# Four graph layers on one core: scores in halves over four banks, weighted sums in one piece, jobs placed by a table

## The chip, the cores and the metric

The kernel runs on one core of one Trainium2 chip. The metric is the device time of one execution in microseconds (us), the median of several runs. One profiled execution is shown beside it, as recorded by the hardware profiler. TensorE is PE in the views, VectorE is DVE, ScalarE is ACT, GpSimd is POOL and SyncE, which here only issues DMAs, is SP.

## The reference

There are 32 batch elements of 512 nodes with 64 features, float32, and one sparse 512x512 matrix `adj`. Four graph layers follow each other, each added to its input after layer norm and relu:

```python
h = relu(layernorm(x)); x = x + L0(h, adj)   # 3 steps: v = relu([v, adj@v] @ W1.T + b1) @ W2.T + b2
h = relu(layernorm(x)); x = x + L1(h, adj)   # 2 steps: z = relu((adj@z) @ W[i])
h = relu(layernorm(x)); x = x + L2(h, adj)   # graph attention, 8 heads of 128, and an output layer of the same form
h = relu(layernorm(x)); x = x + L3(h, adj)   # additive attention

def gat_layer(x, graph, W, b):               # L2: each head, and the output layer
    h = x @ W
    s = einsum('bnd,bmd->bnm', h, h) * graph
    s = where(s == 0.0, -1e16, s)
    a = softmax(s, axis=2)
    return einsum('bnm,bmd->bnd', a, h) + b

# L3: e = leaky_relu(e_src[:, :, None] + e_dst[:, None, :], 0.2) * adj (diagonal 1); softmax; a @ h + bias
```

Almost all the work lies in the attention: for each element eight heads and one output layer of L2, and one of L3, each with a softmax over 512x512 scores.

## The kernel before

**Pairs and units.** Two batch elements (a pair) are worked on together, their 2 x 64 features side by side in 128 partitions. There are 16 pairs. The layers L0 and L1 of a pair are `front(p)`, a Python generator that is advanced step by step. The attention of a pair is cut into ten units: eight `Heads` (element j, two heads each: q = 0 to 3), one `Out` (the output layer of L2 for both elements) and one `Last` (L3). Each unit has a tile `sm` of eight blocks of 128x512 scores.

**What a unit does**, by method:

- `scores(k)`, k = 0 to 3: two blocks. `gram` makes them on TensorE, two banks of `s`, from `Y` (or `HH`) and `ZZ` (L400), and adds -1e16 where the graph has no edge by a bf16 product with `NEGM` (L403). `by_graph` (L417, VectorE) multiplies a block by the graph into `sm` and takes each row's maximum `mx`; `negate` (L424, POOL) makes `nmx` of two blocks. In `Last` the scores come from `pd` (L637) and a Prelu on ACT (L640) writes them into `sm`.
- `exponentials(k)` (L428, ACT): two blocks, with row sums `ssum`.
- `normalise(k)`: a reciprocal of two sums on VectorE (L438), two multiplications on POOL (L440).
- `turn(k)` (L446, VectorE): two blocks are transposed in 32x32 squares.
- `weigh` (L454, TensorE): 16 x 8 matmuls of tiles 32x64 sum the values weighted by the softmax, into four banks `u`. A float32 matmul stands as two instructions in the profile, so a unit has 256.
- Later stages of a `Heads` unit: `evict` (L501, ACT) copies `u` to `us`; `apply_w` multiplies by the head's weights into `py` (L481) and applies a Prelu into `y` (L491); each second unit has `project` (L508, TensorE), whose result is added into `cat` (L517 and L519, VectorE); the last unit of an element has `features` (L524) and `nodes` (L534). `Out` and `Last` have an eviction of their own, then transposes (L551), residual sums, and in `Out` the layer norm and the inputs of `Last`.
- `keys` (L683, TensorE, into `pk`; L691, ACT, into `Y`) prepares the left sides of two units' scores.
- `quarters` issues 16 DMAs on SP that lay values out for `weigh`.

**Groups and lags.** The order of all jobs is written out by hand. Each unit starts at a group number g0, and a tick is four groups. `scores(k)` stands at g0 + k, `exponentials(k)` one later, `normalise(k)` two, `turn(k)` three. `weigh` comes in three chunks of 6, 5 and 5 of its 16 steps at g0 + 9, 10, 11, the eviction and `apply_w` at g0 + 12. A step of the next pair's front stands at certain groups (`FRONT_AT`). Within a group `ORDER` says which kind goes first:

```python
ORDER = ("begin", "norm", "turn", "evict", "s", "keys", "exp", "w", "full", "front", "av", "o")
```

Engines take their instructions in this order, each from its own queue. A pair takes ten ticks; `Out` and `Last` of a pair run among the heads of the next one. The first front runs alone, ahead of everything.

**PSUM.** Eight banks: two for `s` (and `pd`), four in two fixed tiles of two banks (`u`; `py` in the first of them, `pk` in the second), two for all other products (`mm`). `sm` has three buffers.

Of the kernel before, what the change touches and what calls it, by code (L numbers as in the profile page):

```python
# [8 lines left out]
F32 = mybir.dt.float32  # L9
# [5 lines left out]
P = 128  # L15
# [6 lines left out]
def gnn_stack_kernel(  # L22
# [56 lines left out]
    ap_ = ctx.enter_context(tc.tile_pool(name="ap", bufs=3))  # L79
    hp = ctx.enter_context(tc.tile_pool(name="hp", bufs=2))  # L80
    st = ctx.enter_context(tc.tile_pool(name="st", bufs=6))
    ps_s = ctx.enter_context(tc.tile_pool(name="ps_s", bufs=2, space=bass.MemoryType.PSUM))
    ps_u = ctx.enter_context(tc.tile_pool(name="ps_u", bufs=1, space=bass.MemoryType.PSUM))
    ps_m = ctx.enter_context(tc.tile_pool(name="ps_m", bufs=2, space=bass.MemoryType.PSUM))

    def mm_ps():
        return ps_m.tile([P, N], F32, tag="mm", name="mm")

    def two_banks(k, name):

        return ps_u.tile([P, 2, N], F32, tag=f"u{k}", name=name)
# [194 lines left out]
    def aggregated(v, pe, first=True):  # L286

        for m in range(NT):
            if m == 2:
                yield  # L290
            nc.tensor.matmul(  # L291
                pe,
                lhsT=v[:, m].rearrange("p j d -> p (j d)"),
                rhs=AT[:, m, :],
                start=(first and m == 0),
                stop=(m == NT - 1),
            )
# [8 lines left out]
    def front(p, state):  # L306
# [11 lines left out]
        hT = transposed(v, "hT0", 1)  # L318
        yield
        for step in range(STEPS):  # L320

            k = min(step, 1)
            pv = by_nodes(hT, W1T[:, 1, k, :])
            v = lp.tile([P, NT, 2, D], F32, tag="v", name="v")
            if step == 0:
                nc.scalar.copy(v, pv)
            else:
# [5 lines left out]
                )  # L333
            ph = mm_ps()
            nc.tensor.matmul(ph, lhsT=W1T[:, 0, k, :], rhs=hT, start=True, stop=False)  # L335
            yield
            yield from aggregated(v, ph, first=False)
            hT = lp.tile([P, N], F32, tag="hT0", bufs=1, name="hT0")
# [10 lines left out]
        for i in range(LAYERS):  # L349
            pe = mm_ps()  # L350
            yield from aggregated(z, pe)
# [13 lines left out]
        state[p] = {"x2": x2, "z": z, "ZQ": [None, None], "ZZ": [None, None]}  # L365
# [17 lines left out]
    class Unit:  # L383
# [10 lines left out]
        def gram(self, k, operands):  # L394
# [6 lines left out]
            for half in range(2):  # L401
                for ab in range(2):
# [6 lines left out]
                    )  # L409
            for half in range(2):  # L410
                s = 2 * k + half
                self.by_graph(s, pss[half], A2[:, s, :])
            self.negate(k)
# [22 lines left out]
        def normalise(self, k):  # L436
            two = slice(2 * k, 2 * k + 2)
            nc.vector.reciprocal(self.rs[:, two], self.ssum[:, two])  # L438
            for s in range(2 * k, 2 * k + 2):
# [8 lines left out]
        def weigh(self, jbs):  # L448
            if jbs.start == 0:
                self.u = [two_banks(k, "u") for k in range(2)]  # L450
            for jb in jbs:
                for c in range(2):
                    for i in range(4):
                        nc.tensor.matmul(  # L454
                            self.u[i // 2][R[c], i % 2, 0:P],
# [6 lines left out]
    class Heads(Unit):  # L462
# [12 lines left out]
        def apply_w(self):  # L475

            py = two_banks(0, "py")
            for ab in range(2):
                for c in range(2):
                    for r in R:  # L480
                        nc.tensor.matmul(  # L481
                            py[r, c, ab * N // 2 : (ab + 1) * N // 2],
# [4 lines left out]
                        )  # L487
            for ab in range(2):
                h = 2 * self.q + ab
                y = hp.tile([P, 2, N // 2], F32, tag="y", bufs=6, name="y")  # L490
                nc.scalar.activation(  # L491
                    y, py[:, :, ab * N // 2 : (ab + 1) * N // 2], AF.Prelu, bias=cols[:, h : h + 1], alpha=0.01
                )
                state[self.p].setdefault("y", []).append(y.rearrange("p c n -> p (c n)"))

        def stages(self):

            def evict():
                self.us = hp.tile([P, 2, NT // 2, P], F32, tag="us", name="us")
                for ab in range(2):  # L500
                    nc.scalar.copy(self.us[:, ab], self.u[ab][:, :, 0:P])  # L501

            def project():
                s = state[self.p]
                pa = mm_ps()
                for k in range(2):
                    for ab in range(2):
# [6 lines left out]
                        )  # L514
                if self.q == 1:
# [23 lines left out]
            sts = {0: [("evict", evict)]}  # L539
            if self.q % 2 == 1:  # L540
                sts[4] = [("o", project)]
            if self.q == NQ - 1:
                sts[6] = [("full", features)]
                sts[7] = [("full", nodes)]
# [12 lines left out]
    class Out(Unit):  # L557
# [12 lines left out]
        def stages(self):  # L570
            s = state[self.p]

            def evict():

                self.yT = hp.tile([P, N], F32, tag="us", name="yT")
                for ab in range(2):
                    nc.scalar.activation(
                        self.yT[:, ab * N // 2 : (ab + 1) * N // 2].rearrange("p (s i e) -> p i s e", i=2, e=32),
                        self.u[ab][:, :, 0:P].rearrange("p i (s e) -> p i s e", e=32),
# [28 lines left out]
            def nodes():  # L608
# [10 lines left out]

            return {  # L620
                0: [("evict", evict)], 1: [("full", residual)], 2: [("full", norm)], 3: [("full", norm)],
                4: [("full", norm)], 5: [("full", features)], 6: [("full", weights)], 7: [("full", nodes)],
            }

    class Last(Unit):
# [5 lines left out]
        def scores(self, k):  # L631
# [6 lines left out]
            for i in range(2 * k, 2 * k + 2):  # L638
                t = i % NT
                nc.scalar.activation(  # L640
                    self.sm[:, i, :], self.pd[j], AF.Prelu, bias=s["src"][:, t, j : j + 1], alpha=0.2
                )
                self.by_graph(i, self.sm[:, i, :], A3[:, t, :])
            self.negate(k)
# [4 lines left out]
        def stages(self):  # L649
            s = state[self.p]  # L650

            def evict():
                self.yT = hp.tile([P, N], F32, tag="us", name="yT")
                yT = self.yT.rearrange("p (t k i e) -> p k i t e", k=2, i=2, e=32)
                for k in range(2):
                    nc.scalar.activation(
                        yT[:, k],
                        self.u[k][:, :, 0:P].rearrange("p i (t e) -> p i t e", e=32),
# [14 lines left out]
            return {0: [("evict", evict)], 1: [("full", residual)]}  # L673

    def keys(ua, ub):
# [3 lines left out]
        py = two_banks(1, "pk")  # L679
        for ab in range(2):  # L680
            for par in range(2):
                for half, un in enumerate((ua, ub)):
                    nc.tensor.matmul(  # L683
                        py[R[par], half, ab * N // 2 : (ab + 1) * N // 2],
# [4 lines left out]
                    )  # L689
        Y = hp.tile([P, 2, N], F32, tag="Y", name="Y")  # L690
        nc.scalar.copy(Y.rearrange("p u n -> p (u n)"), py.rearrange("p u n -> p (u n)"))  # L691
# [5 lines left out]
    state = {}  # L697
    for _ in front(0, state):
        pass

    LAG_V, LAG_E = 9, 12
    CHUNKS = (range(0, 6), range(6, 11), range(11, 16))
# [105 lines left out]
```

## Time and profile before

| | us |
|---|---|
| median of 3 runs | 2603.95 (2600.87 to 2606.08) |
| the profiled execution: its own time | 2606.89 |
| its span, first to last instruction | 2604.0 |
| PE busy in the span | 2419.7 |
| VectorE busy | 1883.9 |
| ACT busy | 1487.2 |
| POOL busy | 1292.3 |
| granted TensorE clock, mean | 0.972 |

The page of a profile has the busy time of each engine, the span in 40 slices, the DMA queues, the chain of work that ended last (followed back from the last instruction to whatever released each step), and the costliest groups of instructions by line, with the idle time of the engine ahead of them. The timeline lists instructions in order of time, equal ones merged. Matmuls are pipelined, so the length of a group on PE overlaps the next one; the difference of two starts is what a group takes. Busy time per engine by stage, in windows of 156 us between 260 and 2288 us, is nearly constant: PE 149.6 to 150.9, VectorE 116.6 to 119.5, ACT 92.8 to 94.9, POOL 80.7 to 82.2.

### The profile page before, as it was taken

The page shows a single profiled execution, that of the slowest core. Times are in us where ns is not written, and L with a number is a line of the kernel's source. Part 1 is how long each engine was busy: PE and PEld are TensorE (multiplying, and loading weights), DVE is VectorE, ACT ScalarE, POOL GpSimd, SP SyncE. Part 2 cuts the span into 40 slices and gives each one's busy share as a digit, 9 for nine tenths or more (in the row PEclk, how much of TensorE's full clock was granted, in tenths as well). Part 3 has the DMA queues.
Part 4 walks back from the last instruction along what each step waited for, and adds up shares of the span by engine and source line. Part 5 has one row for each costly group of instructions (what it writes and reads, how often), then busy time and mean ns, then how long its engine had stood idle before and what let it go on. Part 6 is the DMA issues. An engine that isn't in the chain of part 4 may idle for free.

```text
span 2604.0 us, 120934 instructions
## 1 busy us (share of the span) xinstructions
PE 2419.7 (93%) x54020; PEld 1340.8 (51%) x54020; DVE 1883.9 (72%) x4390; ACT 1487.2 (57%) x3601; POOL 1292.3 (50%) x2162
## 2 busy tenths in 40 slices
PE   5798999999999999999999999999999999999984
PEld 3344555555555555555555555555555555555552
DVE  3457677877867787786777778677777868778853
ACT  0345565565656556575655656566565655657652
POOL 1335454645545465554545545465554546555522
PEclk9899999999999999999999999999999999999986
DMA  3101011020211102021120201112020110202011
GB/s 77 18 6 27 15 26 32 17 41 12 40 23 25 34 14 41 15 38 25 22 37 10 45 15 34 29 18 40 7 44 19 30 29 14 42 5 43 17 34 26
DMA packets 260748, 70.74 MB, mean 27 GB/s; under 512 B 257660, under 2 KB 258692, under 8 KB 260228
## 3 DMA queue, kind: packets, MB, share of 16 engines
q1 hardware_dynamic: 258944, 62.82, 13.6%
q8 instruction: 422, 6.91, 1.2%
q14 instruction: 98, 0.80, 0.1%
q10 hardware_dynamic: 1284, 0.21, 0.1%
HBM read 8.40 MB, written 4.19 MB: 5 GB/s over the span
## 4 chain that ended last, share of the span: by engine, by line
PE 85%; ACT 7%; DVE 3%; POOL 2%; issue 1%; DMA 1%; SPq 1%; ACTq 0%; POOLq 0%
PE u L454 25%; PE s L400 22%; PE mm L291 12%; PE s L403 5%; PE mm L508 5%; PE mm L303 4%; PE py L481 3%; ACT sm L428 3%; ACT sm L640 2%; PE mm L335 2%; PE pk L683 1%; PE mm L524 1%; PE mm L534 1%; DVE sm L417 1%; POOL r L249 1%; PE mm L551 1%
## 5 line engine op out<-in xcount | busy, mean ns | idle before, releaser
L428 ACT ACTIVATE sm<-sm,nmx 128x512 f32<-128x512 f32 x1280 | 915.0, 721 | 236.7 <-POOL nmx L424 236.7
L417 DVE CUSTOM_DVE_ANT_0 sm<-s,A 128x512 f32<-128x512 f32 x1152 | 744.0, 682 | 360.2 <-PE s L403 359.5
L440 POOL TENSOR_SCALAR sm<-sm,rs 128x512 f32<-128x512 f32 x1280 | 879.5, 700 | 221.7 <-DVE rs L438 218.3
L454 PE MATMUL u<-sm,vq 32*64 32x128 f32 x40960 | 750.2, 282 | 106.4 <-ACT y L491 48.2
L454 PEld LDWEIGHTS u<-sm,vq 32*64 32x64 f32 x40960 | 631.1, 134 | 351.9 <-issue 167.6
L446 DVE STREAM_TRANSPOSE sm<-sm 128x1024 f32<-128x1024 f32 x640 | 784.6, 1226 | 16.3 <-POOL sm L440 15.9
L424 POOL TENSOR_SCALAR nmx<-mx 128x2 f32<-128x2 f32 x640 | 154.0, 241 | 930.4 <-DVE mx L417 589.4
L400 PE MATMUL s<-ZZ,Y 64*64 64x512 f32 x4096 | 603.3, 618 | 13.1 <-DVE mx L417 13.0
L403 PE MATMUL s<-NEGM,I2b 64*64 64x512 bf16 x2304 | 263.3, 379 | 0.0
L428 ACT ACTIVATION_READ_ACCUMULATOR sm<-sm,nmx 128x1 f32 x1280 | 249.8, 195 | 0.0
L400 PEld LDWEIGHTS s<-ZZ,Y 64*64 64x64 f32 x4096 | 127.9, 132 | 189.2 <-DVE mx L417 66.4
L501 ACT COPY us<-u 128x256 f32<-128x256 f32 x256 | 83.4, 381 | 238.8 <-PE u L454 238.8
L291 PE MATMUL mm<-AT,v 128*128 128x512 f32 x384 | 188.2, 614 | 0.0
L438 DVE RECIPROCAL rs<-ssum 128x2 f32<-128x2 f32 x640 | 101.5, 159 | 113.8 <-ACT sm L428 113.0
L491 ACT ACTIVATE y<-py,cols 128x512 f32<-128x512 f32 x256 | 161.7, 685 | 8.2 <-PE py L481 2.8
L403 PEld LDWEIGHTS <-I2b 64*64 64x64 bf16 x2304 | 83.4, 108 | 159.3 <-issue 158.4
L481 PE MATMUL py<-us,Wh 64*64 64x256 f32 x2048 | 136.3, 379 | 5.9 <-ACT us L501 5.9
L291 PE MATMUL mm<-AT,z 128*128 128x512 f32 x256 | 127.3, 622 | 8.1 <-DVE z L253 7.4
L508 PE MATMUL mm<-y,Wo_sb 128*64 128x512 f32 x512 | 124.0, 605 | 0.0
L417 DVE CUSTOM_DVE_ANT_0 sm<-sm,A 128x512 f32<-128x512 f32 x128 | 93.4, 766 | 34.2 <-ACT sm L640 34.2
L249 POOL TENSOR_TENSOR r<-ve,mhalf 128x8 f32<-128x8 f32 x64 | 106.1, 1657 | 22.7 <-DVE ve L247 11.8
L291 PEld LDWEIGHTS mm<-AT,v 128*128 128x128 f32 x384 | 65.5, 189 | 97.7 <-issue 76.7
(124 smaller groups left out, 1870.1 us busy)
## 6 DMA issues: line engine op xcount, KB each, us to landing
vq<-z SPq DMA_DIRECT2D x512, 32.0 KB, 1.9
vq<-hn SPq DMA_DIRECT2D x512, 32.0 KB, 1.9
vq<-h3n SPq DMA_DIRECT2D x512, 32.0 KB, 1.9
xt<-in_x_dram SPq DMA_DIRECT2D x32, 128.0 KB, 3.3
out_dram<-xo SPq DMA_DIRECT2D x32, 128.0 KB, 2.1
A<-in_adj_dram SPq DMA_DIRECT2D x3, 1024.0 KB
Wh<-in_L_gnn_Wh_dram SPq DMA_DIRECT2D x2, 256.0 KB, 3.8
Wo_sb<-in_L_gnn_W_out_dram SPq DMA_DIRECT2D x1, 256.0 KB
```

Of the source, the lines that this page charges most:

```text
L291: nc.tensor.matmul(pe, lhsT=v[:, m].rearrange("p j d -> p (j d)"), rhs=AT[:, m, :], start=(first and m == 0), stop=(m == NT - 1),)
L400: nc.tensor.matmul(pss[half][R[ab], :], lhsT=lhsT, rhs=rhs, start=True, stop=False)
L403: nc.tensor.matmul(pss[half][R[ab], :], lhsT=I2b[R[half], :], rhs=NEGM[R[half], k, :], start=False, stop=True,)
L417: nc.vector.tensor_tensor_reduce(self.sm[:, s, :], src, graph, 1.0, -FMAX, ALU.mult, ALU.max, self.mx[:, s : s + 1])
L424: nc.gpsimd.tensor_scalar(self.nmx[:, two], self.mx[:, two], -1.0, None, ALU.mult)
L428: nc.scalar.activation(self.sm[:, s, :], self.sm[:, s, :], AF.Exp, bias=self.nmx[:, s : s + 1], accum_out=self.ssum[:, s : s + 1],)
L440: nc.gpsimd.tensor_scalar(self.sm[:, s, :], self.sm[:, s, :], self.rs[:, s : s + 1], 1.0, ALU.mult, ALU.mult)
L446: nc.vector.transpose(out=two, in_=two)
L454: nc.tensor.matmul(self.u[i // 2][R[c], i % 2, 0:P], lhsT=self.values(i, c)[32 * i : 32 * i + 32, jb, :], rhs=self.sm[32 * i : 32 * i + 32 ...
L481: nc.tensor.matmul(py[r, c, ab * N // 2 : (ab + 1) * N // 2], lhsT=Wh2[R[c], 2 * self.q + ab, r], rhs=self.us[R[c], ab].rearrange("p i (s ...
L491: nc.scalar.activation(y, py[:, :, ab * N // 2 : (ab + 1) * N // 2], AF.Prelu, bias=cols[:, h : h + 1], alpha=0.01)
L508: nc.tensor.matmul(pa[R[ab], :], lhsT=Wo_sb[:, 2 * (self.q - 1 + k) + ab, :], rhs=s["y"].pop(0), start=(k == 0), stop=(k == 1),)
```

## The change

PSUM is divided otherwise: four banks for `s`, four for `mm`, and `u`, `py` and `pk` are now `mm` tiles of one bank each, in turn with all other products. `sm` has two buffers instead of three. A unit's scores are made in two halves of two Gram products (places s0, s1 and s2, s3); the maxima are jobs of their own, one for each block (r0 to r7). `normalise` takes four blocks with one reciprocal (nA, nB). `weigh` is one piece of 256 instructions, and `aggregated` in the front one piece of four matmuls. Since every tile is one bank, evictions come in more and smaller instructions. `apply_w`, `project` and `keys` become generators, so that the matmuls and the eviction have places of their own (w and y, o and c, k and Y); front steps are split likewise, 25 in all (F0 to F24: F3 transposes, F4 / F7 / F10 the product by nodes, F5 / F8 / F11 its copy, F6 / F9 / F12 the aggregation, F14 and F21 mean and squares, F15 and F22 variance and power). The table `PLACES` gives each job a tick, counted from its unit's or pair's own, and a place within the tick; jobs of a tick run in order of their places. The fronts of the first two pairs run together ahead of everything: seven steps of the second among those of the first. All heads now start at consecutive ticks 0 to 3 and 5 to 8, `Out` of the pair before at tick 4 and `Last` at tick 9. The numbers of matmuls are the same.

```diff
-    ap_ = ctx.enter_context(tc.tile_pool(name="ap", bufs=3))
+    ap_ = ctx.enter_context(tc.tile_pool(name="ap", bufs=2))
...
-    ps_s = ctx.enter_context(tc.tile_pool(name="ps_s", bufs=2, space=bass.MemoryType.PSUM))
-    ps_u = ctx.enter_context(tc.tile_pool(name="ps_u", bufs=1, space=bass.MemoryType.PSUM))
-    ps_m = ctx.enter_context(tc.tile_pool(name="ps_m", bufs=2, space=bass.MemoryType.PSUM))
+    ps_s = ctx.enter_context(tc.tile_pool(name="ps_s", bufs=4, space=bass.MemoryType.PSUM))
+    ps_m = ctx.enter_context(tc.tile_pool(name="ps_m", bufs=4, space=bass.MemoryType.PSUM))
...
         for m in range(NT):
-            if m == 2:
-                yield
             nc.tensor.matmul(
...
             for half in range(2):
-                s = 2 * k + half
-                self.by_graph(s, pss[half], A2[:, s, :])
-            self.negate(k)
+                self.pss[2 * k + half] = pss[half]
+
+        def maxima(self, s):
+            self.by_graph(s, self.pss.pop(s), A2[:, s, :])
+            if s % 2 == 1:
+                self.negate(s // 2)
...
-        def normalise(self, k):
-            two = slice(2 * k, 2 * k + 2)
-            nc.vector.reciprocal(self.rs[:, two], self.ssum[:, two])
-            for s in range(2 * k, 2 * k + 2):
+        def normalise(self, ks):
+            ss = slice(2 * ks.start, 2 * ks.stop)
+            nc.vector.reciprocal(self.rs[:, ss], self.ssum[:, ss])
+            for s in range(ss.start, ss.stop):
...
-        def weigh(self, jbs):
-            if jbs.start == 0:
-                self.u = [two_banks(k, "u") for k in range(2)]
-            for jb in jbs:
+        def weigh(self):
+            self.u = [mm_ps() for _ in range(4)]
+            for jb in range(N // 32):
...
-            py = two_banks(0, "py")
+            py = [mm_ps() for _ in range(2)]
...
+            yield
             for ab in range(2):
...
-                nc.scalar.activation(
-                    y, py[:, :, ab * N // 2 : (ab + 1) * N // 2], AF.Prelu, bias=cols[:, h : h + 1], alpha=0.01
-                )
+                for c in range(2):
+                    nc.scalar.activation(
+                        y[:, c],
+                        py[c][:, ab * N // 2 : (ab + 1) * N // 2],
...
-                for ab in range(2):
-                    nc.scalar.copy(self.us[:, ab], self.u[ab][:, :, 0:P])
+                for i in range(4):
+                    nc.scalar.copy(self.us[:, i // 2, i % 2], self.u[i][:, 0:P])
...
-        nc.scalar.copy(Y.rearrange("p u n -> p (u n)"), py.rearrange("p u n -> p (u n)"))
+        for half in range(2):
+            nc.scalar.copy(Y[:, half, :], py[half])
...
-    state = {}
-    for _ in front(0, state):
-        pass
+    state = {p: {} for p in range(NPAIR)}
+    first, second = front(0, state), front(1, state)
+    HEAD = 7
+    for n, _ in enumerate(first):
+        if 4 <= n < 4 + HEAD:
+            next(second)
+
+    PLACES = {
+        "begin": (0, 0), "s0": (0, 4), "s1": (0, 5), "r0": (0, 6), "r1": (0, 10), "r2": (0, 14),
+        "r3": (0, 16), "x0": (0, 23), "x1": (0, 27), "nA": (0, 45), "s2": (0, 50), "s3": (0, 55),
+        "r4": (0, 57), "r5": (0, 59), "r6": (0, 62), "r7": (0, 63), "x2": (0, 70), "x3": (1, 3),
+        "t0": (0, 66), "t1": (0, 68), "nB": (1, 17), "t2": (1, 43), "t3": (1, 44), "av": (1, 69),
+        "us": (2, 2), "w": (2, 46), "y": (2, 47), "k": (-1, 48), "Y": (-1, 49), "o01": (3, 34),
+        "c01": (3, 38), "o03": (4, 30), "c03": (4, 36), "o11": (3, 12), "c11": (3, 33), "o13": (3, 30),
+        "c13": (3, 35), "f0": (5, 21), "h0": (5, 65), "f1": (5, 28), "h1": (5, 60), "or": (2, 20),
+        "oA": (2, 32), "oB": (2, 49), "oC": (2, 67), "oT": (3, 18), "oW": (3, 54), "oN": (4, 42),
+        "lr": (2, 37), "ZZ1": (0, 9), "ZQ1": (0, 61), "F0": (-2, 30), "F1": (-2, 64), "F2": (-2, 67),
+        "F3": (-1, 11), "F4": (-1, 15), "F5": (-1, 22), "F6": (-1, 40), "F7": (-1, 52), "F8": (-1, 53),
+        "F9": (0, 56), "F10": (2, 7), "F11": (2, 8), "F12": (2, 31), "F13": (3, 26), "F14": (3, 39),
+        "F15": (4, 1), "F16": (4, 29), "F17": (5, 41), "F18": (6, 13), "F19": (6, 51), "F20": (7, 24),
+        "F21": (7, 25), "F22": (7, 58), "F23": (7, 67), "F24": (8, 19),
+    }
...
+    def place(unit, t):
+        at(t, "begin", unit.begin)
+        for k in range(4):
+            at(t, f"s{k}", lambda k=k: unit.scores(k))
+            at(t, f"x{k}", lambda k=k: unit.exponentials(k))
+            at(t, f"t{k}", lambda k=k: unit.turn(k))
+        for s in range(NS):
+            at(t, f"r{s}", lambda s=s: unit.maxima(s))
+        at(t, "nA", lambda: unit.normalise(range(0, 2)))
+        at(t, "nB", lambda: unit.normalise(range(2, 4)))
+        at(t, "av", unit.weigh)
+        for names, fn in unit.stages():
+            parts(t, names, fn)
...
-            for group in ORDER:
-                for gr, fn in todo:
-                    if gr == group:
-                        fn()
-            assert g not in jobs
-            g += 1
+            for _, fn in sorted(jobs.pop(t, []), key=lambda job: job[0]):
+                fn()
+            t += 1
```

## The prediction, made before the changed kernel ran

> **What bounds the kernel now.** I read the page from the top: engines, then the chain that ended last, then TensorE's timeline over one pair of batch elements in the middle, where every pair looks alike.
>
> ```profile
> span 2604.0 us, 120934 instructions
> PE 2419.7 (93%) x54020; PEld 1340.8 (51%) x54020; DVE 1883.9 (72%) x4390; ACT 1487.2 (57%) x3601; POOL 1292.3 (50%) x2162
> ...
> PE 85%; ACT 7%; DVE 3%; POOL 2%; issue 1%; DMA 1%; SPq 1%; ACTq 0%; POOLq 0%
> ...
> L454 PE MATMUL u<-sm,vq 32*64 32x128 f32 x40960 | 750.2, 282 | 106.4 <-ACT y L491 48.2
> ```
>
> TensorE carries 85% of the chain and is busy 93%. The first pd matmuls (L637) of the pairs start 153.3 us apart, almost without scatter: a period is TensorE's own work plus the same few waits. How much is work, how much changing over and how much waiting, only the starts in the timeline tell (columns: start, length, instruction, idle before it and what ended it).
>
> ```profile
> 1598.51 1.04 PE L481 MATMUL py<-us,Wh 64*64 64x256 f32 x16
> 1602.48 2.87 PE L454 MATMUL u<-sm,vq 32*64 32x128 f32 x96 [2.93 <-ACT y L491]
> ...
> 1626.43 0.40 PE L403 MATMUL s<-NEGM,I2b 64*64 64x512 bf16 x4
> 1628.63 1.70 PE L454 MATMUL u<-sm,vq 32*64 32x128 f32 x96 [1.81 <-POOL sm L440]
> ...
> 1662.87 1.65 PE L454 MATMUL u<-sm,vq 32*64 32x128 f32 x96
> 1664.45 1.09 PE L400 MATMUL s<-HH 64*64 64x512 f32 x8
> ...
> 1667.60 1.43 PE L454 MATMUL u<-sm,vq 32*64 32x128 f32 x80
> 1668.96 1.09 PE L400 MATMUL s<-HH 64*64 64x512 f32 x8
> ...
> 1673.51 1.09 PE L400 MATMUL s<-ZZ,Y 64*64 64x512 f32 x8
> 1674.42 0.40 PE L403 MATMUL s<-NEGM,I2b 64*64 64x512 bf16 x4
> 1674.63 1.04 PE L683 MATMUL pk<-ZZ,G 64*64 64x256 f32 x16
> ...
> 1696.02 1.11 PE L400 MATMUL s<-ZZ,Y 64*64 64x512 f32 x6
> 1696.93 0.38 PE L403 MATMUL s<-NEGM,I2b 64*64 64x512 bf16 x2
> 1696.96 0.60 PE L400 MATMUL s<-ZZ,Y 64*64 64x512 f32 x2
> 1697.39 0.38 PE L403 MATMUL s<-NEGM,I2b 64*64 64x512 bf16 x2
> 1697.70 1.43 PE L454 MATMUL u<-sm,vq 32*64 32x128 f32 x80
> ```
>
> From start to start: 96 weighted-sum instructions take 1.58 us (1664.45 - 1662.87), 80 take 1.36. So one costs 13.8 ns, and each chunk 0.25 us on top. A Gram product (L400 with L403) takes 1.24 us between groups of another tile shape, but 1.12 where a group of its own shape follows (1674.63 - 1673.51), and 1.19 where one stands before it. Changing the tile shape is what costs.
>
> Waits in the period from 1596.5: from the start of py to the next start took 3.97 for 0.97 (3.0, the weighted sums waiting for y's eviction), the chunk after it took 2.80 for 1.58 (1.2), one Gram step took 3.06 (1.8, waiting for POOL), one 2.23 (1.0), three took 1.68 instead of 1.24 (1.3: the second of the two s banks comes free late), some slow groups after pauses 0.6. In all about 9. Work is then some 144 of 153.3.
>
> **What the skill says.** The Trainium skill, "TensorEngine Tiling (Array Packing)", Key Properties: changing the tiling mode, not just the tile, drains TensorE. The trace agrees: 0.12 us after a Gram product, 0.25 per chunk. "TensorE: Matmul & The Clock Gate", Part 1: the clock falls back after some 3.4 us idle; the chunk after the 2.93 us pause took 1.8 times its usual length. "ScalarE: Activation LUTs", What ACT_TABLE_LOAD costs: a fixed part for each ACTIVATE, and 0.833 ns an element; here 128x512 copies take 587 ns and 128x256 ones 373 (L536), so 0.84 ns an element, and a fixed part of 0.16 us at most.
>
> **The change, part by part** (all per period; the work is the same: both programs hold equal numbers of matmuls in it).
>
> *Weighted sums in one piece.* Per unit 4.30 us in three chunks become 256 x 13.8 ns + 0.25 = 3.78. Ten units: -5.2.
>
> *Scores in halves.* Two Gram products in a row, 1.12 + 1.19 = 2.31 for 2.48. 18 such pairs: -3.1 at most; some stood beside py or pk already. With four s banks the 1.3 of waiting for the second bank goes too, provided that VectorE has been through.
>
> *Aggregation in one piece.* 2 x 1.91 become 3.63: five times, -1.0.
>
> Counted through the order of TensorE's instructions in both programs, changes of tile shape fall from 94 to 52. With each group's own start-to-start time and its cost of changing, the sum falls from 143.8 to 135.1: -8.7.
>
> *The table and its waits.* The 9 us of waiting depend on the order, so I followed the ten ticks of a period by hand, with times from the timeline: maxima 0.61 each, a transpose of two blocks 1.15, an exponential 0.72, four normalisations on POOL 2.72, mean and squares on POOL 2.1, its power 1.66, handing over 0.1. The tightest loop goes from tick to tick: weighted sums 3.8, their eviction 0.9, last exponentials 1.65 (ACT issues us before x3), reciprocal, four normalisations 2.7, t3 1.25, next weighted sums: 11.1 with the hand-overs. The reciprocal stands behind r3 on VectorE, which makes 11.8. With front or output work between POOL's nB and nA, POOL (nB, squares, nA, power, negation), x2, us and x3 close another loop of 12.6 to 14.3. TensorE's work per tick is 11.7 to 15.7, so mostly it still comes last. I found two places where it doesn't. In tick 2 F11's copy stands between F10 and F12: 0.8. In Last's tick its four first Prelus stand on ACT before the copy of zT, for which F4 waits on TensorE: 2.1; F6 then waits 0.7 for v; the weighted sums wait 0.8 for Y, since they take all four mm banks. Behind the waiting F4 stand all later matmuls of that tick. Together 4.4. The ticks come to 14.5, 11.7, 15.8, 12.5, 12.2, 13.0, 14.5, 14.0, 13.5, 19.3: 141.0. For what such a walk misses I keep -4 to +7.
>
> *What lies beside TensorE.* us becomes four copies for two: 2 x 0.16 more on ACT; y four pieces for two, 0.32; Y two for one, 0.16; Out and Last 0.32 each: at most some 6 us of ACT per period, on top of 94 in 156 (the windows by stage); the trace has no 128x128 copy, and overlapping starts would make it half of that, 3. ACT is at about 70% of 141; what hides it is the Gram pair (2.3) after the weighted sums, during which us (0.9) is made, and without that cover the 6 would count whole. Half the reciprocals go (640 of 159 ns in all become 320): 3 us of VectorE, now about 80%; I count nothing. One sm buffer fewer: r0 of a unit needs the weighted sums two units back, which TensorE has done before that unit's scores: nothing. SP's quarters are moved with their stages: 16 issues of 0.6 us each; after oN's 32, which queue behind F24's 16, the last lands about 10 us before Last's weighted sums. Nothing, but a slower SP queue would show there first.
>
> *Fronts overlapped.* Seven steps of the second front run in the first's waits: about 6 us of TensorE leave the first period, at 2 us more for the head (bounds 0 and 4).
>
> Sum against the profiled execution (span 2604.0, own time 2606.9). Before: head to the first features 84.0, then 126.2, 149.4, 1995.1 (13 periods), 9.5 to the last pd group but one, 133.1 without a front, tail 106.7. After: 86; 126.2 x 141/153.3 - 6, less 2 for waits that a thin period doesn't have, 108; 137; 13 x 141 = 1833; 9; 123 (only 10 us less, as there the loops of 11.8 to 12.6 bind); 100 (coarser halves with four banks: the last Out's scores to its sums some 13 us for 15.8, and fewer waits of av and f; the DMA part stays). Sum 2396. The profiled execution is 3 us above its span and the median of the runs (2603.95) equals the span, so I forecast the same number for the median.
>
> **Rivals.**
>
> 1. Nothing waits (0.12): period 135 to 137; 2396 - 13 x 5 = about 2330. For it: POOL and ACT are at 60 and 70%. Against it: Last's tick.
>
> 2. Half the gain turns into new waits (0.16): VectorE at 80% in strict order, with each copy from mm behind maxima. Period 147 to 151: 2474 to 2526. For it: in the page "DVE sm <- PE s" and "POOL nmx <- DVE mx" are the longest waits, so these queues do wait for each other.
>
> 3. Slower (0.08), by one mechanism: normalising by four closes POOL, VectorE and ACT into the loop that ends at us. It decides once the mean tick passes 15.33 us (153.3/10). At 15.6 it is 2396 + 13 x 15 plus as much in the other stretches, about 2640. It needs 3.8 us more than my 11.8 in every tick; POOL's extra work does that in only three of ten.
>
> 4. The change does not do what it says: the order as built would still have some 94 changes of shape. It has 52, so I give it nothing beyond the 0.02 for no change.
>
> **The numbers.** My case (0.62): 137 to 146 a period, 2345 to 2465. The range takes in part of rivals 1 and 2: 2320 to 2520. Faster by over 0.2% (about what a measurement of this kernel can tell from no change) 0.90, within it 0.02, slower 0.08.
>
> **What would show it.** In the profile after: pd groups 141 us apart; one weighted-sum group of 256 in 3.8 us from start to start; no Gram step of 1.68; in Last's tick idle time before F4's matmul, ended by the copy of zT; ACT's busy share near 70%. Wrong it would be if weighted sums often wait for POOL or VectorE's transposes (rival 3), or if Gram pairs wait for maxima (rival 2).

## The result, and the profile after

The changed kernel is slower: median 2685.06 us of 4 runs (2676.12 to 2688.11) against 2603.80 before, of 4 runs too (2600.87 to 2606.08), a ratio of 1.0307 (95% interval 1.028 to 1.0334). The forecast was 2396. The profiled execution took 2686.01, its span is 2684.2 and its mean granted clock 0.974, as before (0.972).

The starts of the first pd group of each pair (L642 now) cut the span into the stretches of the prediction's sum:

| stretch | before | forecast | after | over forecast |
|---|---|---|---|---|
| start to the first pd group | 369.0 | 340 | 370.8 | 30.8 |
| 13 periods | 1995.1 | 1833 | 2066.2 | 233.2 |
| the period without a front | 133.1 | 123 | 141.5 | 18.5 |
| tail | 106.7 | 100 | 105.7 | 5.7 |

So the loss against the forecast is spread over everything that contains attention. A period is 158.9 us in place of 153.5, and not 141. The page says of what kind it is (engines, chain, groups, DMA queues):

```profile
span 2684.2 us, 121573 instructions
PE 2331.6 (87%) x54020; PEld 1360.6 (51%) x54020; DVE 1883.4 (70%) x4070; ACT 1545.6 (58%) x4241; POOL 1282.7 (48%) x2162
...
q8 instruction: 423, 6.93, 1.1%
...
PE 78%; issue 8%; ACT 5%; DVE 3%; POOL 2%; SPq 2%; DMA 1%; ACTq 0%; POOLq 0%; DVEq 0%
...
L452 PE MATMUL mm<-sm,vq 32*64 32x128 f32 x40960 | 731.1, 276 | 254.0 <-issue 200.0
```

TensorE works less than before (2331.6 for 2419.7): the change did what it says. But 8% of the chain is "issue", 1% before: time in which TensorE waits for nothing that the profile shows. The weighted sums have 200.0 us of it. The list of waits puts it at the head of TensorE's own (columns: us, times, longest):

```profile
PE mm L452 <- issue: 200.0, 157, 2.1
PE mm L452 <- DVE sm L445: 29.9, 5, 12.1
PE mm L297 <- ACT zT L279: 19.6, 14, 1.6
```

Before, the first of these lines read 9.9 us, 14 times. The weighted sums' wait for POOL, 27.1 us before, is 1.8. Two stretches of TensorE's timeline show the new wait (start, length, instruction, idle before it):

```profile
1500.95 3.31 PE L452 MATMUL mm<-sm,vq 32*64 32x128 f32 x215 [0.19 <-DVE v L323]
1505.99 0.87 PE L452 MATMUL mm<-sm,vq 32*64 32x128 f32 x35 [1.72 <-issue]
1506.79 1.09 PE L395 MATMUL s<-ZZ,Y 64*64 64x512 f32 x8
1507.69 0.40 PE L398 MATMUL s<-NEGM,I2b 64*64 64x512 bf16 x4
1507.91 1.04 PE L395 MATMUL s<-ZZ,Y 64*64 64x512 f32 x8
1508.77 0.40 PE L398 MATMUL s<-NEGM,I2b 64*64 64x512 bf16 x4
1509.10 0.66 PE L369 MATMUL mm<-ident,z 128*128 128x128 f32 x4
...
1533.15 2.99 PE L452 MATMUL mm<-sm,vq 32*64 32x128 f32 x192
1537.67 1.21 PE L452 MATMUL mm<-sm,vq 32*64 32x128 f32 x64 [1.52 <-issue]
1538.81 1.09 PE L395 MATMUL s<-ZZ,Y 64*64 64x512 f32 x8
```

The Gram pair takes 2.31 us (1509.10 - 1506.79), exactly as forecast. The weighted sums take 5.66 (1538.81 - 1533.15) where 3.78 was forecast: they stop once, in the middle of a piece, for 1.5 us. Over the 130 pieces of the 13 periods the mean is 5.74 and the median 5.64. Steps of more than 0.4 us from one weighted-sum matmul to the next number 7 in the 13 periods before (6.6 us) and 157 after (218.0 us). Per period that is 16.8 us, and what remains of the period is 142.2, close to the forecast's 141.0.

### The profile page after: what moved, and what is told of

Same layout as the page of the kernel before. It is cut to its first block, busy times and chain, and to the rows that moved or that the text cites. A ratio compares the mean times of both kernels' runs of the same rounds, so it can differ in the third digit from the quotient of the medians.

```text
span 2684.2 us, 121573 instructions
## 1 busy us (share of the span) xinstructions
PE 2331.6 (87%) x54020; PEld 1360.6 (51%) x54020; DVE 1883.4 (70%) x4070; ACT 1545.6 (58%) x4241; POOL 1282.7 (48%) x2162
## 4 chain that ended last, share of the span: by engine, by line
PE 78%; issue 8%; ACT 5%; DVE 3%; POOL 2%; SPq 2%; DMA 1%; ACTq 0%; POOLq 0%; DVEq 0%
PE mm L452 24%; PE s L395 19%; PE mm L285 10%; PE mm L479 5%; PE s L398 4%; PE mm L297 4%; PE mm L512 3%; SPq L267 2%; PE mm L690 2%; POOL sm L439 2%; PE mm L331 2%; DVE sm L416 1%; ACT sm L427 1%; PE mm L539 1%; ACT sm L644 1%
## 5 line engine op out<-in xcount | busy, mean ns | idle before, releaser
L427 ACT ACTIVATE sm<-sm,nmx 128x512 f32<-128x512 f32 x1280 | 913.8, 720 | 526.4 <-POOL nmx L423 524.5
L416 DVE CUSTOM_DVE_ANT_0 sm<-s,A 128x512 f32<-128x512 f32 x1152 | 726.1, 683 | 374.9 <-PE s L398 374.9
L452 PE MATMUL mm<-sm,vq 32*64 32x128 f32 x40960 | 731.1, 276 | 254.0 <-issue 200.0
L452 PEld LDWEIGHTS mm<-sm,vq 32*64 32x64 f32 x40960 | 631.5, 132 | 388.6 <-issue 276.7
L395 PE MATMUL s<-ZZ,Y 64*64 64x512 f32 x4096 | 554.6, 600 | 10.3 <-issue 6.9
L398 PE MATMUL s<-NEGM,I2b 64*64 64x512 bf16 x2304 | 243.8, 377 | 2.8 <-issue 2.7
L491 ACT ACTIVATE y<-mm,cols 128x256 f32<-128x256 f32 x512 | 199.4, 471 | 24.6 <-PE mm L479 24.6
L505 ACT COPY us<-mm 128x128 f32<-128x128 f32 x512 | 99.2, 278 | 160.0 <-PE mm L452 159.7
L479 PE MATMUL mm<-us,Wh 64*64 64x256 f32 x2048 | 140.3, 389 | 0.8 <-ACT us L505 0.8
L245 POOL TENSOR_TENSOR r<-ve,mhalf 128x8 f32<-128x8 f32 x64 | 106.1, 1658 | 36.2 <-DVE ve L243 35.5
L479 PEld LDWEIGHTS mm<-us,Wh 64*64 64x64 f32 x2048 | 66.3, 132 | 95.2 <-ACT sm L427 58.5
L416 DVE DVE_READ_ACCUMULATOR2_ANT mx<- 128x1 f32 x1280 | 105.4, 82 | 0.0
```

The costliest lines, as they stand in the source:

```text
L395: nc.tensor.matmul(pss[half][R[ab], :], lhsT=lhsT, rhs=rhs, start=True, stop=False)
L398: nc.tensor.matmul(pss[half][R[ab], :], lhsT=I2b[R[half], :], rhs=NEGM[R[half], k, :], start=False, stop=True,)
L416: nc.vector.tensor_tensor_reduce(self.sm[:, s, :], src, graph, 1.0, -FMAX, ALU.mult, ALU.max, self.mx[:, s : s + 1])
L427: nc.scalar.activation(self.sm[:, s, :], self.sm[:, s, :], AF.Exp, bias=self.nmx[:, s : s + 1], accum_out=self.ssum[:, s : s + 1],)
L452: nc.tensor.matmul(self.u[i][R[c], 0:P], lhsT=self.values(i, c)[32 * i : 32 * i + 32, jb, :], rhs=self.sm[32 * i : 32 * i + 32, c * NT : ( ...
L479: nc.tensor.matmul(py[c][r, ab * N // 2 : (ab + 1) * N // 2], lhsT=Wh2[R[c], 2 * self.q + ab, r], rhs=self.us[R[c], ab].rearrange("p i (s ...
```

## The experiments

**The theories.** A: the pauses are TensorE's instructions arriving late. The queue named "instruction" moves 423 packets of 16 KB in the profile after; 108,040 matmuls and weight loads in 423 packets are 255.4 each, so a packet carries 256 instructions. The "256 instructions" of a unit's weighted sums count the matmuls alone; with their weight loads they are 512, two packets. Numbering TensorE's instructions by the trace's order, 126 of the 139 pauses over 0.6 us in the 13 periods end at the same place of a block of 256 (193 or 194), and 126 end 1.1 to 1.7 us after a packet of this queue has landed, where a tenth of all moments lie so. The Trainium skill, "Runtime: NRT & Kernel Launch", Terms, says that each engine's instruction RAM is refilled in 16 KiB blocks, which the packets agree with; how fast, it does not say. The same page, Instruction fetch mechanics, has 256 instructions to a block, as here, and calls the cost of crossing a block's end mostly hidden; if A is right, it isn't in this kernel. B: they are waits for a bank or a transfer that the trace doesn't show. C: TensorE's clock is throttled.

**A bare stream of matmuls.** The kernel leaves the whole computation out: weighted-sum matmuls alone, on fixed data, with and without 128x512 products between them.

```diff
+        wide(8)          # 128x512 products, each two matmuls in the profile
+        sums(64)         # 1024 matmuls of 32x64 tiles, 128 columns, densely
+        wide(12)
+        sums(32, 512)    # 512 with 512 columns
+        for gap in (2, 4, 6, 8, 10, 12):
+            wide(12)
+            for _ in range(6):
+                sums(16) # 256
+                wide(gap)
```

> This kernel computes nothing of the reference: it copies x to the output and runs bare TensorE streams with no waits between them: 512 small matmuls of the weighted sums' form (tile 32x64, 128 columns) without a break, then 256 of 512 columns, then pieces of 128 small ones with 2 to 12 wide matmuls (128x128, 512 columns) between pieces, then pieces of 40 with 1 wide one. Theory A (the instruction stream of TensorE is brought in blocks of 256 instructions and short instructions use a block up faster than the next one comes): the dense stream shows a pause of 1 to 2.5 us at each 256th instruction, counted over weight loads and matmuls, though nothing waits on data; the stream of 512 columns shows none, or shorter ones; the pauses shrink as the wide matmuls between pieces grow. Theory B (the pauses come from waits of the kernel, on banks, values or other engines, that the trace does not name): no pause here, 13.8 ns an instruction throughout. Theory C (a throttle of the clock after dense work): pauses at intervals of time, not at an instruction count.

TensorE's timeline in this kernel:

```profile
26.31 2.08 PE L74 MATMUL bank<-xs 32*64 32x128 f32 x128 [1.75 <-issue]
29.76 2.08 PE L74 MATMUL bank<-xs 32*64 32x128 f32 x128 [1.37 <-issue]
33.22 2.08 PE L74 MATMUL bank<-xs 32*64 32x128 f32 x128 [1.37 <-issue]
36.67 2.08 PE L74 MATMUL bank<-xs 32*64 32x128 f32 x128 [1.37 <-issue]
```

Bursts of exactly 128 matmuls, with their weight loads 256 instructions, then a pause of 1.37: 3.45 us from burst to burst. No other engine works here, no bank is waited for, and the granted clock is 1.0. B and C fall. All 38 pauses of this kernel end 1.1 to 1.7 us after an instruction packet has landed. With 512 columns there is no pause at all. Of the 36 pieces of 256 matmuls, the piece of the changed kernel, 31 pause once, at the second block's end within the piece. A's expectation that the pauses shrink with more wide products ahead did not come true: in the group with 12 (10.57 us) five of six still pause, for 0.90 to 1.20 us. The five of the 36 that run through have the first block's end within their first 16 matmuls and at least six wide products ahead of them; they take 3.80, the price that was forecast.

**How dense is too dense.** The same without computation: pieces of 128, 96 and 64 matmuls, each followed by one wide product; bf16 in place of float32; 256 columns.

```diff
+        for n in (8, 6, 4):      # 128, 96, 64 matmuls
+            for _ in range(12):
+                sums(n)
+                wide(1)
+            wide(12)
+        sums(128, P, xb)         # bf16
+        wide(12)
+        sums(64, 256)            # 256 columns
```

> Bare TensorE streams again, nothing of the reference is computed. Theory A with the number measured in the first stream run (a block of 256 instructions every 3.45 us): where the instructions of a block last t, the stream pauses 3.45 - t at each block. Pieces of 128 small matmul instructions with one wide matmul between (about 3.0 us for 260 instructions): pauses of 0.3 to 0.6. Pieces of 96 (2.6 us for 196, so 3.45 for 256): none or 0.1. Pieces of 64 (2.2 us for 132, 4.2 for 256): none. bf16 operands (one weight load and one matmul for each product, 1024 products): 128 of them to a block as before, so pauses at each 128th matmul. 256 columns: 128 last about 3.5 us, so hardly a pause. If the pauses went by time or by work, bf16 would show them at other counts.

The timeline, first pieces of 128, then the bf16 stream:

```profile
72.34 2.49 PE L77 MATMUL bank<-xs 32*64 32x128 f32 x128
74.76 1.12 PE L87 MATMUL bank<-xs 128*128 128x512 f32 x2
75.82 0.91 PE L77 MATMUL bank<-xs 32*64 32x128 f32 x39
77.26 1.59 PE L77 MATMUL bank<-xs 32*64 32x128 f32 x89 [0.54 <-issue]
...
202.20 1.93 PE L77 MATMUL bank<-xb 32*64 32x128 bf16 x128 [2.17 <-issue]
205.93 1.93 PE L77 MATMUL bank<-xb 32*64 32x128 bf16 x128 [1.79 <-issue]
```

A piece of 128 with its wide product is 260 instructions and takes 3.48 us (75.82 - 72.34): 3.43 for 256. Where no pause is named, the piece is stretched (2.49 for 2.1). Pieces of 96 take 2.64 for 196 instructions, 3.45 for 256, with a few stretched. Pieces of 64 take 2.19 for 132, 4.25 for 256, and do not pause. Nor do 256 columns, where 128 matmuls last about 3.5. The bf16 stream pauses as float32 does: it is the count of instructions, not the work in them. From 200.3 us on the granted clock is half in this stream, and a burst takes 1.93 in place of 1.29; the bursts start 3.45 to 3.73 apart all the same, so the clock does not set the distance. So the limit lies at about 3.45 us for each 256 instructions, and in a dense stream the crossing of a block's end is not hidden.

**Weighted sums in halves.** The changed kernel with `weigh` in two pieces of 128 and the first Gram product of the next scores between them.

```diff
-        "av": (1, 69), "us": (2, 2),
+        "av0": (1, 69), "av1": (2, 4.5), "us": (2, 4.7),
...
+    PIECES = (range(0, 8), range(8, 16))
```

> The changed kernel with the weighted sums of a unit in two halves, the first Gram product of the next unit between them; everything else keeps its place, but the eviction us follows the second half. Theory A: a half is 256 instructions, the Gram product gives the fetch 1.1 us; most pauses inside L452 go (178 of over 0.6 us with 276 us in all before), against one more chunk (0.25 us) and one Gram pair broken (0.17) per unit, 65 us in all: 2450 to 2560. Theory B, or loops through POOL, VectorE and ACT bound the tick: 2680 to 2750, the idle time of TensorE only moves to other lines.

Measured: 2544.43, ratio to before 0.9758 (0.9742 to 0.9775). TensorE's timeline and waits:

```profile
1532.32 2.10 PE L453 MATMUL mm<-sm,vq 32*64 32x128 f32 x128
1534.35 1.09 PE L395 MATMUL s<-ZZ,Y 64*64 64x512 f32 x8
1535.26 0.40 PE L398 MATMUL s<-NEGM,I2b 64*64 64x512 bf16 x4
1535.59 2.19 PE L453 MATMUL mm<-sm,vq 32*64 32x128 f32 x128
1537.71 1.09 PE L395 MATMUL s<-ZZ,Y 64*64 64x512 f32 x8
```

```profile
PE mm L453 <- issue: 21.0, 44, 1.7
PE mm L277 <- ACT us L506: 20.7, 14, 1.6
```

(`us` in such lines is the tile of copied sums, not microseconds.) The same 256 matmuls take 2.03 and 2.12 here, and a half 2.29 in the median of the run. From the first half to the end of the second it is 5.39 us with the Gram product in between, less than the 5.66 of the one piece: the Gram product fills the time of the pause. The steps over 0.4 us in the 13 periods fall from 218.0 us to 42.6, and the period from 158.9 to 150.2, although a chunk more per unit, a broken Gram pair and a new wait of 1.5 per period for `us` have come in. More changes of shape, less time: that one edit of places turns the change from a loss into a gain shows that the piece's length decided.

**In thirds**, with a Gram product after each of the first two, as the kernel before had its chunks:

```diff
-        "av0": (1, 69), "av1": (2, 4.5), "us": (2, 4.7),
+        "av0": (1, 69), "av1": (2, 4.5), "av2": (2, 5.5), "us": (2, 5.7),
...
-    PIECES = (range(0, 8), range(8, 16))
+    PIECES = (range(0, 6), range(6, 11), range(11, 16))
```

> The changed kernel with the weighted sums in three pieces (192, 160, 160 instructions counting weight loads as well), the two first Gram products of the next unit between them; the eviction us follows the third. Theory A: hardly any pause is left; 276 us come back, three chunks cost 0.5 us a unit more than one and broken Gram pairs 0.17, 107 us in all: 2500 to 2560. Theory B or loops: 2700 and more.

Measured: 2664.36, ratio 1.0223 (1.0208 to 1.0238): far over what was expected. TensorE's waits:

```profile
PE mm L277 <- ACT us L506: 40.7, 27, 3.1
PE mm L513 <- ACT us L506: 12.6, 18, 2.8
PE mm L369 <- ACT us L506: 11.8, 28, 0.5
```

The pauses are down again (35.5 us in 13 periods), but the period is 157.1. With the last piece behind the second Gram product, nothing of the unit covers the eviction `us` any more, and TensorE's next product stands waiting for the banks that it has to empty. All its waits for `us` sum to 86 us, where halves had 28 (20.7 of it in L277). TensorE is also busy 53 us longer than in halves (2421.2 for 2368.2). That is 111 of the 116 us between the two spans (2659.2 and 2543.1). Why it is busy longer is only argued: a third chunk per unit, and pieces that are stretched without a named wait.

**The kernel before, with its chunks joined** (all 16 steps at g0 + 11):

```diff
-    LAG_V, LAG_E = 9, 12
-    CHUNKS = (range(0, 6), range(6, 11), range(11, 16))
+    LAG_V, LAG_E = 11, 12
+    CHUNKS = (range(0, 16),)
```

> The kernel before with one edit: the weighted sums of a unit in one piece of 512 instructions, at the place of the last chunk. Theory A: pauses of 1.2 to 1.8 us appear in each unit, 160 of them: some 2604 - 83 (chunks saved) + 240 = 2700 to 2800. Theory B or loops of the new table: no pauses, 2604 - 83, so 2500 to 2560.

Measured: 3011.83, ratio 1.155 (1.1518 to 1.1581), more than any theory had. TensorE's waits:

```profile
PE s L400 <- DVE mx L417: 150.6, 147, 3.3
PE u L454 <- issue: 148.3, 128, 1.9
```

The pauses appear in the old kernel too, with its own banks and order (148.3 for 9.9). They are 138 of the 408 us by which the span grew. Another 136 have another cause: with two s banks, the chunks had been filling the time in which VectorE frees a bank (150.6 for 15.0). And TensorE is busy 160.8 us longer (2580.5 for 2419.7) at a lower granted clock (0.940 for 0.972); why the clock is lower was not tested. So the old chunks did two things, of which the page of before shows neither as a wait.

**Halves, and Last's Prelus taken out of ACT's way.** The prediction had found that the first Prelus of `Last` delay the copy of zT. They are issued with their maxima here.

```diff
-            for i in range(2 * k, 2 * k + 2):
-                nc.scalar.activation(
-                    self.sm[:, i, :], self.pd[j], AF.Prelu, bias=s["src"][:, i % NT, j : j + 1], alpha=0.2
-                )
 
         def maxima(self, i):
+            s = state[self.p]
+            j = i // 4
+            nc.scalar.activation(
+                self.sm[:, i, :], self.pd[j], AF.Prelu, bias=s["src"][:, i % NT, j : j + 1], alpha=0.2
+            )
```

> The version with the weighted sums in halves around the first Gram product, and one more edit: in the unit Last each Prelu stands with its block's maximum instead of four of them ahead of the copy of zT. If the waits of TensorE in Last's tick are ACT's order (zT behind the Prelus, us behind two of them), 1.5 to 3.5 us per pair go: 2490 to 2525, after 2544. If they are something else: 2540.

Measured: 2530.93, ratio 0.972 (0.9704 to 0.9736), a little over the expected range; period 148.9. In halves the two Prelus of Last's first scores stood ahead of `us`, and the delay showed as the wait of L277 for `us` (20.7) instead of that for zT. Neither is left among TensorE's longest waits, and the 13 periods are 17.6 us shorter than in halves, 1.35 each. The medians of these two versions differ by 13.5 us, less than the changed kernel's own medians did between jobs (20 us, below), so it is the wait that shows the gain, 20.7 us down to 4.1. This version beats both kernels.

**Halves around the second Gram pair**, in the version just shown, so that `us` keeps its cover and the scores their pair:

```diff
-        "av0": (1, 69), "av1": (2, 4.5), "us": (2, 4.7),
+        "av0": (1, 49.9), "av1": (1, 69), "us": (2, 2),
```

Seven of the front's and output's jobs are moved ahead of av0, since it takes all four mm banks.

> The same, but the halves of the weighted sums stand around the second pair of Gram products (av, s2, s3, av), which stay together, and us is hidden behind the next pair again; the front's and output's matmuls of the tick's second part move ahead of the first half. Theory A: a block then holds a Gram pair of 2.3 us, lasts over 4 us and causes no pause; per unit it costs one chunk (0.25) over one piece. Sum per pair 135.1 + 2.5, with 4 to 10 for waits on mm banks and on transposes, 142 to 148: 2420 to 2510. If VectorE, which gets the second scores 2 us later, binds instead: 2520 to 2600.

Measured: 2888.09, ratio 1.1095 (1.1079 to 1.1112), against both expectations. Waits of this kernel, and one weighted-sum piece in its timeline:

```profile
ACT sm L427 <- POOL nmx L423: 1002.3, 259, 8.4
DVE sm L416 <- PE s L398: 618.8, 173, 8.0
PE mm L453 <- ACT y L492: 66.4, 68, 3.8
```

```profile
1526.18 4.80 PE L453 MATMUL mm<-sm,vq 32*64 32x128 f32 x128 [1.24 <-POOL sm L439]
1530.92 1.09 PE L395 MATMUL s<-HH 64*64 64x512 f32 x8
```

VectorE waits for scores 618.8 us where it was 374.9 in the changed kernel, and ACT 1002.3 for POOL where it was 524.5 (247.3 and 519.9 in the version that this one starts from). The pauses did go, as theory A had it (29.4 us of "issue" in the weighted sums). But half the weighted sums stand before the second scores now, wait there for the sum's banks (y) and for POOL, and, as the order has it, hold up the scores, on which the whole unit's maxima and exponentials hang. How the 357 us divide among these waits was not worked out. The granted clock was lower, too: 0.943 in the mean, and half from 1527.3 to 1530.7, inside the piece shown. That is some 1.7 of the 2.7 us that it takes more than 2.03; the first six steps, 1.28 us together, are most of the rest.

**The overlapped fronts**, undone in the changed kernel, in the best one, and once more in the changed kernel beside an unedited copy of it on the same chip:

```diff
-    HEAD = 7
+    HEAD = 0
```

> The changed kernel without the overlap of the first two fronts: the first runs alone, all steps of the second stand in the table. The traces show the head 7 us longer with the overlap (first features at 91.1 us for 84.0) and the stretch after it 11 us shorter (115.2 for 126.2, of which part is the table's). If the overlap is worth what was forecast (6 us gained, 2 lost), this is 0 to 5 us slower than the changed kernel; if its cost in the head is 7, it is 1 to 5 us faster: 2680 to 2690 either way.

> The version with halves around the first Gram product and Last's Prelus at their maxima, without the overlap of the first two fronts. In the changed kernel the overlap cost 8 us in the head (first features at 91.1 us with it, at 83.0 without) and, without it, pauses at instruction blocks were 22 us fewer, which may be chance of where blocks end. If only the head counts: 2515 to 2526, after 2531; if the pauses fall again: 2495 to 2515; if the second front's steps are missed later: above 2531.

> The changed kernel once more, in one job with the version without the overlapped fronts, since the two were measured in different jobs. The instruction blocks' packets took 1.14 us on average in the first profile of the changed kernel and 1.07 to 1.08 in the later jobs. If pauses depend on that, it now gives 2660 to 2678 with pauses of 250 to 265 us; if not, 2680 to 2690 as before.

> The changed kernel without the overlap of the first two fronts, beside the changed kernel in one job. If the overlap costs its 8 us in the head: 5 to 10 us below it; if the front's steps weigh as much when the table has to take them: equal within 4; if the 23 us seen between jobs are the overlap's: 20 to 25 below.

Measured: 2662.47 without the overlap, ratio 1.0228 (1.0211 to 1.0244); in the best version 2536.56, 0.9738 (0.9722 to 0.9754), which is not better than 0.972. The first alone would have said that the overlap costs 23 us. Side by side it is nothing: 2664.91 with it (1.0224, 1.0202 to 1.0246) and 2665.68 without (1.0224, 1.0195 to 1.0252). The 20 us between the first runs of the changed kernel and this copy lie between runs at different times. In the profiles 15.8 of them are in steps over 0.4 us of the weighted sums (285.1 for 269.3). The instruction packets took 1.14 us on average in the first profile and 1.05 to 1.10 in later ones, which fits a kernel that waits for them, and the copy came out as expected for that case (260.4 us in pauses over 0.6 us); that this is the cause was not tested further.

## Why the prediction was wrong

**The step that failed** is the first of its parts: "4.30 us in three chunks become 256 x 13.8 ns + 0.25 = 3.78". The 13.8 ns came from the difference between chunks of 96 and 80, and was carried to 256. There it does not hold: the 130 pieces of the 13 periods take 5.74 each, with 218.0 us of pauses, 1.7 a piece. The term was to bring -5.2 per period and brought +14, ten times 5.74 - 4.30.

The trace of before could have told. It holds pieces over 96: one of 160 in each of 15 pairs, which takes 2.47 to 4.32 us where 13.8 ns each and 0.25 make 2.46, and five whole units in one piece, from 2502 us on. Two of them (columns as above):

```profile
1759.75 2.50 PE L454 MATMUL u<-sm,vq 32*64 32x128 f32 x157
1763.71 0.43 PE L454 MATMUL u<-sm,vq 32*64 32x128 f32 x3 [1.45 <-issue]
...
2514.16 3.42 PE L454 MATMUL u<-sm,vq 32*64 32x128 f32 x225
2518.91 0.69 PE L454 MATMUL u<-sm,vq 32*64 32x128 f32 x31 [1.32 <-issue]
2520.14 1.52 PE L481 MATMUL py<-us,Wh 64*64 64x256 f32 x16 [0.54 <-ACT us L501]
```

The second is the changed kernel's piece: 256 matmuls with one "issue" pause, 5.98 us from start to start (0.54 of it a wait of L481). And the page of before names the instruction queue, whose 422 packets the prediction did not relate to 54,020 matmuls and as many weight loads.

**What was right.** With the pauses taken off, the period is 142.2 for 141.0.
- Gram pair 2.31, as forecast; the steps of 1.68 us for a second bank are gone.
- Aggregation in one piece: 3.63 us (1546.69 - 1543.06), as forecast. It has only long matmuls, and does not pause.
- F4 waits for zT, as forecast, by 1.4 a period for 2.1; with the Prelus moved, the best version has neither this wait nor the one that took its place.
- ACT is busy 58.4 us longer, 3.65 a pair (3 to 6 forecast), half the reciprocals went (50.0 us for 101.5), and neither became the bound.
- The rest of the walk through the ticks, that VectorE and POOL close no loop beyond TensorE's work, holds in the sum; its single waits of 0.7 and 0.8 were not looked for one by one.
- One reading goes past the page that the prediction cites for the clock: the clock was at 0.51 from 1602.4 to 1605.5, after a pause of 2.93 us, less than the 3.4 that the page has.

**The head.** Forecast was a gain of 6 us for 2 lost. Measured is nothing in the sum: the first features come at 91.1 us (forecast 86). In the two kernels measured side by side they come at 90.2 with the overlap and 84.8 without, the first pd groups at 368.1 and 372.2, and the medians are the same. The stretch up to there is 30.8 over the forecast, of which its pauses explain 25.7 (27.9 for 2.2 before).

**The rivals.** The result lies on the slower side that was given 0.08, but not by its mechanism: rival 3 had the weighted sums wait for POOL, and that wait shrank. Nor was it new waits for VectorE (rival 2). Without the pauses the whole would be near 2420 (2684.2 less 285.1 in all steps over 0.4 us, with the 22.8 of before put back), inside the forecast's range; this sum was not run, as no version keeps one piece without pauses. The five unpaused pieces of 3.80 in the bare stream are the nearest to it. That TensorE can do the same work without most of the pauses, and what that then costs in chunks and broken pairs, the halves show: 2544 and 2531, 61 and 74 us under before, where 208 was forecast.

## What to carry to other kernels

Before short TensorE instructions are joined into longer runs, count them, weight loads too, against time: in these runs TensorE got at most 256 instructions in each 3.45 us, and what had been fetched ahead seldom carried a run of 512 short ones to its end. Long matmuls between the short ones give the fetch time, so a "cost of changing" may be paying for something; two pieces of half the length around one Gram product beat both the one piece and the three. And when a piece is moved, keep what covers its eviction and what its place had been filling: thirds, and halves moved earlier, lost 120 and 357 us against the halves in place that they start from, with almost the same work. Look, too, for the longest run of the kind that the trace of before already holds: here it had the pause.

## What the runs showed of the hardware

- TensorE's instructions arrive in packets of 16 KB, 256 instructions; a dense stream of 32x64 tiles with 128 columns runs in bursts of 256, one each 3.45 us (some 3.73), with 1.37 us or more of it idle. That is 27 ns a matmul, where the chunks of the kernel before show 13.8. The packets start 3.44 to 3.80 us apart there, though each takes 1.05 us on average; what fills the rest was not found.
- The number of instructions decides, not their work: bf16 pauses as float32 does, 256 and 512 columns do not.
- More than 10 us of long matmuls ahead of a piece of 256 seldom saves it: five of six pause once all the same. In the two bare streams a packet started only when 300 instructions or fewer were left ahead of the place where the stream would have to stop, so a longer wait fetches nothing more. A pause ends 1.1 to 1.7 us after an instruction packet has landed (all 38 in the first bare stream).
- The profile calls this wait "issue". Short of a pause, it can show as a stretched group with no wait named (128 in 2.49 us for 2.1).
- A group can also be stretched by the clock: at half the granted clock eight weighted-sum matmuls take 220 ns (in the 4.80 us piece), where 13.8 ns each make 110.
